# Projecting queries and keys without padding, in a transformer block with two mixtures of experts

## The chip, the cores and the metric

The kernel runs on one NeuronCore of a Trainium2 chip. The metric is device time in microseconds from one launch. Before the change it is 3325.41 us, the median of three runs (3321.82 to 3326.35).

The engines are named as in the profile: PE multiplies matrices (PEld is its weight load), DVE and ACT work elementwise and reduce, POOL also sends indirect transfers, SP only issues transfers. ACT and SP each have a queue of transfers of their own, and each queue works in the order in which it was written.

## The reference, cut to what matters

The input x has 4096 tokens of 256 values. The block is feed-forward, attention, feed-forward, each added to x:

```python
x = x + 0.5 * ffn(layernorm(x))
x = x + attn(layernorm(x))
x = x + 0.5 * ffn(layernorm(x))
```

Attention has 16 heads of 16 values, over all 4096 tokens:

```python
qkv = einsum('bsd,ed->bse', x, qkv_w) + qkv_b      # 3 x 16 heads x 16
scores = einsum('bhqe,bhke->bhqk', q, k) * 0.25
out = einsum('bhqk,bhke->bhqe', softmax(scores), v)
out = einsum('bsd,ed->bse', out, proj_w) + proj_b
```

The feed-forward part routes each token to 4 of 32 experts and adds a shared expert. Everything is fp32.

## The kernel before, in words

The program has five stages: the front of the first layer (`first_front`: normalize, route, shared expert), its experts, the projections to queries, keys and values, attention (into which the front of the second layer is laced in small pieces), and the second layer's experts with the final sums. In `projections` and in `attention` the order on PE, ACT, DVE and SP is the order in which the code is written (`tc.manual_schedule`); POOL's is not fixed so.

**Layout by groups.** A head's 16 values are padded to 32 rows (`HP`), so that four heads fill 128 partitions: a group g of `NG = 4`. The host lays the weights out in this way, with zeros in the padding. Row 16 of each head (`HD`) has a purpose: for keys its weight is 0 and its bias 1.0, for queries it is 0 and later takes a shift, so that the score matmul adds the shift. `kT` holds all keys so padded, 128 x 4 x 4096, in SBUF. The queries go to DRAM as `qd`, one 128 x 512 block for each chunk and group.

**`projections`** works through eight chunks (c) of 512 tokens (`QB`). For a chunk:

- `begin(c)`, on DVE, adds the five results of each token (four experts, shared) with L767, four tiles of 128 tokens, normalizes them (L141 to L167) and gives the rows. Each tile's results come by a fetch on SP (L907, 640 KB); there are six buffers, and the fetch for tile t+6 follows the sums of tile t. POOL then adds the projection's bias to x (L923) and stores it (L926).
- `turned` (L177) transposes the rows on PE; ACT copies them to `xT` (L180).
- `queries_or_keys(c, i, xT)`, i = 0 for queries and 1 for keys: for each of the four groups, two accumulating matmuls (L935), then on ACT the bias and the copy out (L948) and the square (L952). Queries are stored to `qd` from ACT's queue (L950); keys are written straight into `kT`.
- `norms` sums the squares by head with a matmul of 32 output columns for each group (L960); DVE takes the maximum (L967).
- `values` multiplies for v (L974); DVE adds the bias, a tile broadcast to all partitions, and writes v, 17 values for a head, the last one being 1 (L982).
- DVE sums `xT` over the chunk (L1003), for the mean of the keys.

In the code the order is transposes(c), queries(c), `begin(c+1)`, keys(c), norms of the queries, values, norms of the keys. So DVE makes the rows of the next chunk while PE works on this one.

After the last chunk a chain of small steps (L1011 to L1057) finds the mean key (L1019, L1031) and a bound on the scores, from which the shift follows, and a flag. If the flag is set, `take_maxima` finds exact maxima.

**`attention`** goes over 8 chunks of queries, 4 groups and 32 key tiles. At its start DVE clears PSUM banks (L1161), SP loads the first query block (L1165) and the first block of x (L1174), DVE adds the shift (L1170), and PE begins with L1183. Later loads are written two steps into the group before.

Weights for `projections` are loaded on ACT's queue at its start: wqk (L886, 1 MB), wv (L891, two transfers in 64-byte runs), the value bias bv (L898, broadcast), the projection bias (L902).

Of the kernel before, what the change touches and what calls it, by code (L numbers as in the profile page):

```python
# [9 lines left out]
F32 = mybir.dt.float32  # L10
# [49 lines left out]
def kernel(  # L60
# [29 lines left out]
    x1_at = x1[:].rearrange("(t p) d -> p t d", p=P)  # L90
    qd = dram.tile([NQB, NG, P, QB], F32, name="qd")

# [683 lines left out]
    def first_front(layer, keep):  # L776
        n = layer.n
        with (
# [31 lines left out]
            for ch in range(2, nch):  # L810
                load(ch, n)

            routes = [layer.route(ch, xts[ch], pool, pm) for ch in range(nch)]
            xTs = []
# [60 lines left out]
    def projections(layer, side):  # L875
# [4 lines left out]
        with (  # L880
# [3 lines left out]
        ):  # L884
            wqk_sb = pool.tile([P, NC, 2 * NG * P], F32, name="wqk_sb", bufs=1)
            nc.scalar.dma_start(  # L886
                wqk_sb[:], wqkv[:, : 2 * NG * P].rearrange("(c p) e -> p c e", p=P)
            )
            wv_sb = pool.tile([P, NC, NH, HD], F32, name="wv_sb", bufs=1)
            for c in range(NC):  # L890
# [5 lines left out]
                )  # L896
            bv_sb = pool.tile([P, NH, HP], F32, name="bv_sb", bufs=1)
            nc.scalar.dma_start(  # L898
                bv_sb[:].rearrange("p h r -> p (h r)"), bv.to_broadcast([P, NH * HP])
            )  # L900
            bproj_sb = pool.tile([P, D], F32, name="bproj_sb", bufs=1)
# [27 lines left out]
            def queries_or_keys(c, i, xT):  # L929

                squares = []
                for g in range(NG):
                    ps = pm.tile([P, QB], F32, tag="m", name="qk_ps")
                    for cc in range(NC):
                        nc.tensor.matmul(  # L935
                            ps[:],
                            wqk_sb[:, cc, (i * NG + g) * P : (i * NG + g + 1) * P],
                            xT[:, cc, :],
                            start=(cc == 0),
                            stop=(cc == NC - 1),  # L940
                        )
                    bias = bqk_sb[:, i * NG + g : i * NG + g + 1]
                    if i == 0:
                        q = pool.tile([P, QB], F32, tag="q", name="q", bufs=3)
                        part = q[:]
                    else:
                        part = kT[:, g, c * QB : (c + 1) * QB]
                    nc.scalar.activation(part, ps[:], AF.Identity, bias=bias)  # L948
                    if i == 0:
                        nc.scalar.dma_start(qd[c, g], part)  # L950
                    sq = pool.tile([P, QB], F32, tag="sq", name="sq", bufs=2 * NG - 2)
                    nc.scalar.activation(sq[:], ps[:], AF.Square, bias=bias)  # L952
                    squares.append(sq)
                return squares

            def norms(c, i, squares):

                ps = pm.tile([P, QB], F32, tag="m", name="sq_ps")
                for g in range(NG):
                    nc.tensor.matmul(  # L960
                        ps[g * HP : (g + 1) * HP, :],
                        of_head2,
                        squares[g][:],
                        start=True,
                        stop=True,
                    )
                nc.vector.tensor_reduce(norm[:, i, c : c + 1], ps[:], AX.X, ALU.max)  # L967

            def values(c, xT):
                for t in range(0, QT, 2):  # L970
                    ps = pm.tile([P, 2, D], F32, tag="m", name="v_ps")
                    for a in range(2):
                        for cc in range(NC):
                            nc.tensor.matmul(  # L974
                                ps[:, a, :],
                                xT[:, cc, (t + a) * P : (t + a + 1) * P],
                                wv_sb[:, cc].rearrange("p h r -> p (h r)"),
                                start=(cc == 0),
                                stop=(cc == NC - 1),
                            )  # L980
                    for a in range(2):
                        nc.vector.tensor_tensor(  # L982
                            v[:, c * QT + t + a, :, 0:HD],
                            ps[:, a, :].rearrange("p (h r) -> p h r", r=HD),
                            bv_sb[:, :, 0:HD],
                            ALU.add,
                        )

# [3 lines left out]
            for c in range(NQB):  # L992
                xT = pool.tile([P, NC, QB], F32, tag="xT", name="xT")
                for _ in turned(pm, rows, QT, xT, nc.scalar.copy):
                    pass
# [6 lines left out]
                norms(c, 1, k2)  # L1002
                nc.vector.tensor_reduce(sums[:, :, c : c + 1], xT[:], AX.X, ALU.add)  # L1003

# [10 lines left out]
            nc.vector.tensor_scalar(mean_in[:], mean_in[:], 1.0 / T, None, ALU.mult)  # L1015
            ps = pm.tile([P, NG], F32, tag="m", name="kmean_ps")
            for g in range(NG):
                for cc in range(NC):
                    nc.tensor.matmul(  # L1019
                        ps[:, g : g + 1],  # L1020
                        wqk_sb[:, cc, (NG + g) * P : (NG + g + 1) * P],
                        mean_in[:, cc : cc + 1],
                        start=(cc == 0),
                        stop=(cc == NC - 1),
                    )
            mean = small.tile([P, NG], F32, name="mean")
            nc.vector.tensor_add(mean[:], ps[:], bqk_sb[:, NG:])
            nc.vector.tensor_mul(mean[:], mean[:], mean[:])
            ps = pm.tile([P, 1], F32, tag="m", name="mean_ps")
            for g in range(NG):  # L1030
                nc.tensor.matmul(  # L1031
                    ps[g * HP : (g + 1) * HP, :],
                    of_head2,
                    mean[:, g : g + 1],
                    start=True,
                    stop=True,
                )
# [20 lines left out]
        return shift, flag  # L1058

    def take_maxima(kT):  # L1060


        with (
# [3 lines left out]
            for b in range(NQB):  # L1067
                for g in range(NG):
                    q = pool.tile([P, QB], F32, tag="q", name="q")
                    nc.sync.dma_start(q[:], qd[b, g])  # L1070
                    for t in range(QT):
# [25 lines left out]
                        cols = slice(t * P, (t + 1) * P)  # L1097
                        nc.vector.tensor_add(q[:, cols], q[:, cols], tp[:])
                    nc.sync.dma_start(qd[b, g], q[:])

# [48 lines left out]
    def attention(layer, kT, v, shift, keep):  # L1149
# [5 lines left out]
        with (  # L1155
# [5 lines left out]
            nc.vector.memset(pm.all[:, Banks.RING :, :], 0.0)  # L1161

            def load_queries(b, g):
                q = pool.tile([P, QB], F32, tag="q", name="q", bufs=3)
                nc.sync.dma_start(q[:], qd[b, g])  # L1165
                qs[b, g] = q
# [152 lines left out]
    for base, step, sign in ((0, -HP, 1), (HD - 1, HP, -1)):  # L1319
# [8 lines left out]
        )  # L1328
    of_head2 = of_head[:].rearrange("p j r -> p (j r)")

# [108 lines left out]
```

## Time and profile before

| What | Value |
|---|---|
| Median of 3 runs | 3325.41 us |
| The profiled execution | 3322.82 us |
| Its span, first to last instruction | 3321.1 us |
| PE busy | 3061.0 us, 92% |
| ACT busy | 2334.0 us, 70% |
| DVE busy | 979.0 us, 29% |
| POOL busy | 615.0 us, 19% |
| Granted TensorE clock, mean | 0.957 |

The profile comes from one execution. Its page gives the busy time of each engine, groups of instructions by line with count, busy time and mean duration, the idle time before them with what ended it, and the chain of work that ended last. Other views of the same trace give the busy time of each engine in a stretch, the instructions in order of time, and who waited for whom. Times in them count from the start of the span. Idle time of an engine costs nothing unless the work behind it is what ends the kernel, so each stage has to be read on its own.

### The profile page before, as it was taken

The numbers are of one execution on the slowest core, as the hardware profiler recorded it, in microseconds if no ns is written. First come the engines' busy times: TensorE is split into PE (matmuls) and PEld (weight loads), VectorE is DVE, ScalarE is ACT, GpSimd is POOL, SyncE is SP. The second block draws the span as 40 slices with busy tenths as digits, with TensorE's granted clock in tenths as the row PEclk, the third lists the DMA queues.
The fourth block names the chain that finished last, engine by engine and source line by source line (L and its number), as shares of the span: only waits on it lengthen the run. The fifth ranks groups of instructions, "written<-read, shape, count | busy, mean of one in ns | idle before, by whom it ended". The sixth has DMA issues, their size and how long they took to land.

```text
span 3321.1 us, 50114 instructions
## 1 busy us (share of the span) xinstructions
PE 3061.0 (92%) x20183; PEld 1060.6 (32%) x20183; DVE 979.0 (29%) x2837; ACT 2334.0 (70%) x3753; POOL 615.0 (19%) x644
## 2 busy tenths in 40 slices
PE   5769969989999999999999999999999999958990
PEld 3446644422222222222222222222222222225660
DVE  6734447601012112202211210221121122033447
ACT  2112215579999898898999989999998988932220
POOL 3757741100001000100100010010010001015771
PEclk7879989989999999999999999999999999979995
DMA  6358865333100000000000010000000000007878
GB/s 245 132 176 272 275 224 205 122 125 99 59 4 31 17 7 4 27 20 4 30 20 4 12 35 4 7 27 20 4 30 17 7 4 27 7 19 242 275 237 320
DMA packets 131217, 282.21 MB, mean 85 GB/s; under 512 B 23568, under 2 KB 71312, under 8 KB 130576
## 3 DMA queue, kind: packets, MB, share of 16 engines
q1 hardware_dynamic: 83840, 165.84, 14.6%
q0 software_dynamic: 31872, 97.56, 8.4%
q10 hardware_dynamic: 15248, 15.38, 1.4%
q8 instruction: 163, 2.67, 0.3%
q14 instruction: 94, 0.77, 0.1%
HBM read 146.64 MB, written 132.06 MB: 84 GB/s over the span
## 4 chain that ended last, share of the span: by engine, by line
PE 76%; DVE 3%; issue 1%; DMA 0%; SPq 0%; POOL 0%; ACT 0%; DVEq 0%; POOLq 0%
PE banks L1183 33%; PE banks L1201 30%; PE h L720 4%; PE o L742 2%; PE banks L375 2%; DVE xt L767 2%; PE xbt_ps L694 1%; PE banks L1275 1%; PE banks L395 1%; PE banks L230 1%; PE banks L177 0%; PE banks L273 0%; DMA xb<-xg 0%; DMA y<-ys 0%; DVE den L1224 0%
## 5 line engine op out<-in xcount | busy, mean ns | idle before, releaser
L1193 ACT ACTIVATE ex<-banks 128x512 f32<-128x512 f32 (+1 forms) x3223 | 2055.9, 715 | 164.0 <-PE banks L1183 128.5
L1183 PE MATMUL banks<-q,kT 32*128 32x512 f32 x8192 | 1178.3, 641 | 11.2 <-DVE q L1170 9.9
L1201 PE MATMUL banks<-ex,v 128*17 128x512 f32 x8192 | 1079.2, 598 | 0.0
L350 POOL DMA_INDIRECT xg<-xr,sidx x256 | 247.8, 968 | 2275.7 <-DVE beyond L343 2161.7
L1183 PEld LDWEIGHTS banks<-q,kT 32*128 32x128 f32 x8192 | 327.6, 183 | 846.2 <-ACT ex L1193 704.4
L1201 PEld LDWEIGHTS banks<-ex,v 128*17 128x17 f32 x8192 | 136.1, 95 | 778.1 <-issue 777.1
L1221 DVE COPY o<-banks 128x512 f32<-128x512 f32 x32 | 22.1, 692 | 1186.1 <-PE banks L1201 647.9
L750 POOL DMA_INDIRECT ys<-yb,toi x304 | 292.5, 962 | 138.0 <-issue 78.0
L720 PE MATMUL h<-xT,w 128*128 128x512 f32 x512 | 232.1, 596 | 0.0
L700 ACT COPY xT<-xbt_ps 128x512 f32<-128x512 f32 (+1 forms) x112 | 50.6, 452 | 137.4 <-PE xbt_ps L694 105.5
L746 ACT COPY yb<-o 128x512 f32<-128x512 f32 x64 | 37.5, 585 | 136.6 <-PE o L742 94.9
L729 ACT ACTIVATE s<-h 128x512 f32<-128x512 f32 (+1 forms) x112 | 51.5, 460 | 102.5 <-PE h L720 102.5
L720 PEld LDWEIGHTS h<-xT,w 128*128 128x128 f32 x512 | 93.2, 192 | 92.8 <-issue 92.8
L742 PE MATMUL o<-w,hT 128*128 128x256 f32 x512 | 121.1, 379 | 0.0
L935 PE MATMUL qk_ps<-xT,wqk_sb 128*128 128x512 f32 x256 | 113.8, 603 | 1.7 <-ACT xT L180 1.7
L1224 DVE RECIPROCAL den<-den 128x512 f32<-128x512 f32 x32 | 107.3, 3353 | 1.1
L731 DVE TENSOR_TENSOR hT<-s,h 128x512 f32<-128x512 f32 (+1 forms) x112 | 57.8, 516 | 163.1 <-PE h L720 156.8
L742 PEld LDWEIGHTS o<-w,hT 128*128 128x128 f32 x512 | 93.6, 190 | 17.5 <-issue 7.7
L767 DVE SCALAR_TENSOR_TENSOR xt<-y,wk,xt 128x256 f32<-128x256 f32 x192 | 95.1, 495 | 6.9
L694 PE MATMUL xbt_ps<-ident,xb 128*128 128x128 f32 x512 | 71.2, 283 | 28.0 <-DMA xb<-xg 28.0
L698 DVE COPY xT<-xbt_ps 128x512 f32<-128x512 f32 (+1 forms) x112 | 58.1, 518 | 82.2 <-PE xbt_ps L694 61.6
L694 PEld LDWEIGHTS xbt_ps<-ident,xb 128*128 128x128 f32 x512 | 62.3, 145 | 37.0 <-issue 25.0
(221 smaller groups left out, 1761.3 us busy)
## 6 DMA issues: line engine op xcount, KB each, us to landing
y<-ys SPq DMA_DIRECT2D x64, 640.0 KB, 7.1
xb<-xg SPq DMA_DIRECT2D x62, 528.0 KB, 6.4
w<-in_wexp_dram SPq DMA_DIRECT2D x64, 384.0 KB, 4.1
xg<-zeros SPq DMA_DIRECT2D x152, 132.0 KB, 2.2
xg<-zero SPq DMA_DIRECT2D x32, 264.0 KB, 4.4
qd<-q ACTq DMA_DIRECT2D x32, 256.0 KB, 5.0
q<-qd SPq DMA_DIRECT2D x32, 256.0 KB, 2.6
xbb<-xg SPq DMA_DIRECT2D x48, 132.0 KB, 4.6
```

The source lines that it names most:

```text
L350: ins = nc.gpsimd.indirect_dma_start(out=self.xg[:], out_offset=bass.IndirectOffsetOnAxis(ap=self.sidx[:, t0 + t, k : k + 1], axis=0), in_ ...
L375: nc.tensor.matmul(ps[:], ws13_sb[:, c, h0 : h0 + P], xT[:, c, i0 * P : (i0 + QT) * P], start=(c == 0), stop=(c == NC - 1),)
L694: nc.tensor.transpose(tp[:, i * P : (i + 1) * P], xb[:, i, c * P : (c + 1) * P], ident[:])
L720: nc.tensor.matmul(ps[:, : n * P], w[:, (j * NC + c) * H : (j * NC + c + 1) * H], xT[:, c, : n * P], start=(c == 0), stop=(c == NC - 1),)
L742: nc.tensor.matmul(o[:, i, :], hT[:, (i0 + i) * P : (i0 + i + 1) * P], w2, start=True, stop=True)
L750: ins = nc.gpsimd.indirect_dma_start(out=ys[:], out_offset=bass.IndirectOffsetOnAxis(ap=b["toi"][:, i : i + 1], axis=0), in_=yb[:, i, :], ...
L767: nc.vector.scalar_tensor_tensor(xt, y[:, k, :], self.wk[:, t, k : k + 1], y[:, K, :] if k == 0 else xt, ALU.mult, ALU.add,)
L935: nc.tensor.matmul(ps[:], wqk_sb[:, cc, (i * NG + g) * P : (i * NG + g + 1) * P], xT[:, cc, :], start=(cc == 0), stop=(cc == NC - 1),)
L1183: nc.tensor.matmul(pm.all[:, banks[j], :], kT[rows, g, t * P : (t + 1) * P], q[rows, :], start=True, stop=True,)
L1193: nc.scalar.activation(ex[:, i : i + n, :], pm.all[:, k : k + n, :], AF.Exp, scale=SCALE)
L1201: nc.tensor.matmul(acc[j * HP : j * HP + HV, :], v[:, t, g * HG + j, :], ex[:, j, :], start=(t == 0), stop=(t == NT - 1),)
L1224: nc.vector.reciprocal(den[:], den[:])
```

## The change

Queries and keys are projected without padding. Two groups (2h and 2h+1, a half h of `NG // 2 = 2`) share one matmul: the columns of the weights are placed so that rows j*32 to j*32+15 of the output belong to the first group's head j and rows j*32+16 to j*32+31 to the second's.

- The weights come by 16 transfers on ACT's queue, each taking the 64 real columns of a group and half of the contraction.
- The biases are rearranged on DVE with a shuffle and three elementwise steps.
- `qd` is stored by head with 17 rows; row 16 is zeroed by one transfer at the kernel's start. A query block is stored on SP's queue, twice a chunk, and read by four transfers of 17 rows into a tile whose other rows have been cleared; three fixed tiles take turns.
- Keys: ACT first fills the chunk of `kT` with the column that has 1.0 in row 16 of each head, and then eight transfers on SP's queue spread the 16-row pieces into `kT`.
- `norms` uses a matmul of 64 output columns for each half.
- The value bias is added by a matmul with one row of ones; ACT instead of DVE copies v out.
- The sum of `xT` comes from ACT's copy of the transposed rows, by its accumulator.
- `of_both` is built on POOL at the kernel's start.

```diff
-    qd = dram.tile([NQB, NG, P, QB], F32, name="qd")
+    qd = dram.tile([NQB, NG // 2, 2 * HG, HV, QB], F32, name="qd")
...
+            nc.sync.dma_start(
+                qd[:].rearrange("b h k r q -> (b h k) r q")[:, HD, :], zero[:, :QB]
+            )
...
-            wqk_sb = pool.tile([P, NC, 2 * NG * P], F32, name="wqk_sb", bufs=1)
-            nc.scalar.dma_start(
-                wqk_sb[:], wqkv[:, : 2 * NG * P].rearrange("(c p) e -> p c e", p=P)
-            )
+            wqk_sb = pool.tile([P, NC, 2, NG // 2, P], F32, name="wqk_sb", bufs=1)
+            for cc in range(NC):
+                for a in range(2):
+                    for g in range(NG):
+                        h, i = divmod(g, 2)
+                        first_col = (a * NG + g) * P
+                        nc.scalar.dma_start(
+                            wqk_sb[:, cc, a, h].rearrange("p (j i d) -> p i j d", j=HG, i=2)[:, i],
+                            wqkv[
+                                cc * P : (cc + 1) * P, first_col : first_col + P
+                            ].rearrange("p (j r) -> p j r", j=HG)[:, :, :HD],
+                        )
...
+            nc.vector.stream_shuffle(
+                swapped[:], bqk_sb[:], [(r + HD) % HP for r in range(HP)]
+            )
...
+            nc.vector.tensor_scalar(bias_sb[:], first_bias, low_half[:], None, ALU.mult)
+            nc.vector.scalar_tensor_tensor(
+                bias_sb[:], second_bias, high_half[:], bias_sb[:], ALU.mult, ALU.add
+            )
...
+            nc.vector.tensor_scalar(one_row[:], behind[:], SCALE, None, ALU.mult)
...
-            bv_sb = pool.tile([P, NH, HP], F32, name="bv_sb", bufs=1)
+            bv_sb = pool.tile([1, NH, HD], F32, name="bv_sb", bufs=1)
+            nc.scalar.dma_start(bv_sb[:], bv.rearrange("o (h r) -> o h r", r=HP)[:, :, :HD])
...
             def queries_or_keys(c, i, xT):
+                cols = slice(c * QB, (c + 1) * QB)
+                if i == 1:
+                    nc.scalar.activation(
+                        kT[:, :, cols],
+                        zeros[:, 0:1].unsqueeze(2).to_broadcast([P, NG, QB]),
+                        AF.Identity,
+                        bias=one_row[:],
+                    )
                 squares = []
-                for g in range(NG):
+                part = pool.tile([P, NG // 2, QB], F32, tag="q", name="q", bufs=3)
+                for h in range(NG // 2):
                     ps = pm.tile([P, QB], F32, tag="m", name="qk_ps")
                     for cc in range(NC):
                         nc.tensor.matmul(
                             ps[:],
-                            wqk_sb[:, cc, (i * NG + g) * P : (i * NG + g + 1) * P],
+                            wqk_sb[:, cc, i, h],
                             xT[:, cc, :],
...
+                    nc.scalar.activation(part[:, h, :], ps[:], AF.Identity, bias=bias)
                     if i == 0:
-                        q = pool.tile([P, QB], F32, tag="q", name="q", bufs=3)
-                        part = q[:]
-                    else:
-                        part = kT[:, g, c * QB : (c + 1) * QB]
-                    nc.scalar.activation(part, ps[:], AF.Identity, bias=bias)
-                    if i == 0:
-                        nc.scalar.dma_start(qd[c, g], part)
+                        nc.sync.dma_start(qd[c, h, :, :HD, :], part[:, h, :])
...
+                if i == 1:
+                    by_group = kT[:].rearrange("p (h i) t -> p h i t", i=2)
+                    for r in range(0, P, HD):
+                        j, k = r // HP * HP, r % HP // HD
+                        nc.sync.dma_start(
+                            by_group[j : j + HD, :, k, cols], part[r : r + HD, :, :]
+                        )
...
-                for g in range(NG):
+                for h in range(NG // 2):
                     nc.tensor.matmul(
-                        ps[g * HP : (g + 1) * HP, :],
-                        of_head2,
-                        squares[g][:],
+                        ps[h * 2 * HP : (h + 1) * 2 * HP, :],
+                        of_half,
+                        squares[h][:],
...
+                        nc.tensor.matmul(
+                            ps[:, a, :],
+                            ones[0:1, :],
+                            bv_sb[:].rearrange("o h r -> o (h r)"),
+                            start=True,
+                            stop=False,
+                        )
...
-                    for a in range(2):
-                        nc.vector.tensor_tensor(
-                            v[:, c * QT + t + a, :, 0:HD],
-                            ps[:, a, :].rearrange("p (h r) -> p h r", r=HD),
-                            bv_sb[:, :, 0:HD],
-                            ALU.add,
-                        )
+                    t0 = c * QT + t
+                    nc.scalar.copy(
+                        v[:, t0 : t0 + 2, :, 0:HD],
+                        ps[:].rearrange("p a (h r) -> p a h r", r=HD),
+                    )
...
-                for _ in turned(pm, rows, QT, xT, nc.scalar.copy):
+                sums_of = iter([sums[:, cc, c : c + 1] for cc in range(NC)])
+                for _ in turned(
+                    pm,
+                    rows,
+                    QT,
+                    xT,
+                    lambda out, ps: nc.scalar.activation(
+                        out, ps, AF.Identity, accum_out=next(sums_of)
+                    ),
+                ):
                     pass
...
-                nc.vector.tensor_reduce(sums[:, :, c : c + 1], xT[:], AX.X, ALU.add)
...
+    def read_queries(q, b, g):
+        for j in range(HG):
+            nc.sync.dma_start(q[j * HP : j * HP + HV, :], qd[b, g // 2, 2 * j + g % 2])
...
+            q_tiles = [pool.tile([P, QB], F32, name=f"q{i}", bufs=1) for i in range(3)]
+            for q in q_tiles:
+                nc.vector.memset(q[:], 0.0)
+
             def load_queries(b, g):
-                q = pool.tile([P, QB], F32, tag="q", name="q", bufs=3)
-                nc.sync.dma_start(q[:], qd[b, g])
+                q = q_tiles[(b * NG + g) % 3]
+                read_queries(q, b, g)
                 qs[b, g] = q
...
-    of_head2 = of_head[:].rearrange("p j r -> p (j r)")
+    of_both = const.tile([P, 2, HG, HP // HG], F32, name="of_both")
+    nc.gpsimd.memset(of_both[:], 1.0)
+    for base, step, sign in ((0, -1, 1), (HD - 1, 1, -1)):
+        nc.gpsimd.affine_select(
...
+    of_half = of_both[:].rearrange("p i j r -> p (i j r)")
```

The matmuls for the mean key (L1019, L1031) go over the halves in the same way, and `take_maxima` reads its queries by `read_queries` and stores only its row of maxima.

## The prediction

> **What bounds the kernel now.** I read the page's chain first. It says PE 76%, nearly all of it in attention (L1183, L1201), and its pieces reach back only to 678 us, so it says nothing of the projection stage that the change rewrites (about 476 to 681 us):
>
> ```profile
> 678.05 0.02 SPq L1165
> 678.07 0.04 issue
> 678.11 2.72 DMA q<-qd
> ```
>
> The stage is therefore read from the busy time by stretch (columns: PE, weight loads, DVE, ACT, POOL, then granted clock, DMA share, GB/s):
>
> ```profile
> 476.00:497.00 21.00, 1.39 (x5) 0.97 (x6) 13.28 (x42) 0.00 (x0) 0.24 (x1) 0.50 0.84 318
> 539.00:560.00 21.00, 20.76 (x77) 10.17 (x79) 16.77 (x47) 11.28 (x18) 3.11 (x2) 1.00 0.56 202
> 560.00:581.00 21.00, 20.76 (x77) 10.22 (x80) 16.81 (x48) 11.39 (x18) 3.11 (x2) 1.00 0.57 203
> 665.00:682.00 17.00, 4.21 (x36) 3.52 (x32) 5.92 (x21) 1.49 (x2) 0.37 (x1) 0.61 0.14 38
> ```
>
> In steady state PE is busy 20.76 of 21.0 us at full clock: **PE is the bound of this stage**, DVE second with 16.8, ACT 11.3. Ahead of it PE waits 20 us for the first rows; behind it 16 us pass in small serial steps. The groups by line in 476 to 682 us give the terms:
>
> ```profile
> L935 PE MATMUL qk_ps<-xT,wqk_sb 128*128 128x512 f32 x256 | 113.8, 603 | 1.7 <-ACT xT L180 1.7
> L974 PE MATMUL v_ps<-wv_sb,xT 128*128 128x256 f32 x128 | 29.8, 386 | 0.0
> L960 PE MATMUL sq_ps<-sq,of_head 128*32 128x512 f32 x128 | 17.1, 605 | 0.0
> L982 DVE TENSOR_TENSOR v<-v_ps,bv_sb 128x256 f32<-128x256 f32 x32 | 12.1, 420 | 16.8 <-PE v_ps L974 16.8
> L1003 DVE TENSOR_REDUCE sums<-xT 128x2 f32<-128x1024 f32 x8 | 9.7, 1210 | 0.0
> L1019 PE MATMUL kmean_ps<-mean_in,wqk_sb 128*128 128x1 f32 x16 | 3.0, 315 | 2.4 <-DVE mean_in L1015 2.4
> ```
>
> The projection matmuls wait 1.7 us in all, so what PE no longer does comes off the clock until the next engine is reached.
>
> **PE per chunk.** The last chunk in order of time: transposes begin at 644.57, L935 at 645.90, norms at 659.83, values at 660.83, norms at 664.48, end 665.55. So a chunk is 1.33 + 13.93 + 1.00 + 3.65 + 1.00 = 20.91 us. Half the query and key matmuls go: 6.97 instead of 13.93. The value bias adds four K=1 matmuls of 256 columns, eight records; sixteen such records of L974 take 3.65, so +1.82 (a contraction of one row streams as many columns; no row says that it is cheaper). Norms: two matmuls of 64 output columns instead of four of 32. Four of 32 run beside each other (eight records in 1.00 us); if two of 64 do so too, still 1.00; one after another 2 x 0.87 = 1.74, +0.74 twice. I take 1.00, nearest the row. The transposed copy now also sums (no row; 0 to 0.3 us for each of two, partly under the first matmul): +0.15. **PE chunk 15.9 us** (15.8 to 17.4).
>
> **DVE per chunk.** It loses L982 and L1003. One round of sums and normalizing for the next chunk runs from 583.80 to 597.65, 13.85 us; two norm reductions add 1.2. But now there is no slack behind it, and POOL's addition L923 starts as soon as xn is done. Order of time, first chunk:
>
> ```profile
> 496.76 2.37 POOL L923 TENSOR_TENSOR xt<-xt,bproj_sb 128x1024 f32<-128x1024 f32 x1 [28.72 <-PE tp L177]
> 496.95 3.50 DVE L767 SCALAR_TENSOR_TENSOR xt<-y,wk,xt 128x256 f32<-128x256 f32 x3
> ```
>
> Three L767 that otherwise take 1.53 took 3.50: the line's longest instruction is 2.46 us against 0.485, so DVE stood still until POOL was done. In later chunks PSUM reductions and waits lay there and nothing was lost; now the next round's L767 meet it. DVE's loop is 2.45 (end of xn to end of POOL, 597.65 to 600.10) + 13.85 - 0.2 = **16.1 us**, a hair above PE. If the collision vanished, PE's 15.9 would rule.
>
> **ACT per chunk** loses four query/key pairs and its query DMA issues, and gains a fill of kT of 128x2048 (a 512 step is 0.57 us: about 1.9) and two copies for values (0.6 each): 1.2 + 8 x 0.57 + 1.9 + 1.2 = 8.9 us. It is free before the next transposed copy; without that cover the fill would cost 1.9 a chunk.
>
> **SP and the transfers.** Per chunk SP issues 4 fetches, 2 query stores and 8 key transfers, 14 x 0.33 = 4.6 us. The queue is in order, so the fetches of one round now stand behind the next chunk's two query stores (ready 5.6 us into it) and the eight key transfers. A fetch is used about 15 us later and lands in 6.4; cover enough. Bytes per chunk: 4 x 0.655 + 0.5 + 0.5 + 0.5 = 4.2 MB, over 16.1 us 261 GB/s. The 202 of today is demand, as this stretch shows:
>
> ```profile
> 488.00:490.00 2.00, 0.00 (x0) 0.00 (x0) 1.86 (x5) 0.00 (x0) 0.00 (x0) 0.50 1.01 412
> ```
>
> In attention SP loads queries up to two groups ahead (it waits 1269.9 us in all at L1165 for PE to free a tile), so 128 transfers instead of 32 are hidden there.
>
> **The start of the stage.** One 1 MB load becomes 16 of 32 KB in 64-byte runs, on ACT's queue ahead of wv, bv, bproj, and ahead of ACT's first copy at 497.14. The nearest row is eight 32 KB loads at the kernel's start:
>
> ```profile
> 2.35 11.08 ACTq L129 DMA_DIRECT2D wproj_sb<-in_wproj_dram  x8
> ```
>
> 1.39 us each, though one issue takes 0.32. The issues' records name eight completion semaphores, handed out in turn over both queues, so the ninth transfer waits for the first to land, even one of the other queue; SP's list of waits shows it:
>
> ```profile
> SPq L802 <- DMA wproj_sb<-in_wproj_dram: 4.0, 3, 2.7
> ```
>
> 20 issues x 1.39 = 27.7 from 465.28: 493. Against that, the Trainium skill (DMA: Bandwidth & Descriptors, Rules for kernel authors) says to coalesce: under 64 KB one pays mostly overhead. With the roughly 2 us fixed cost that the page fits on another issuing path, paid 20 times, the estimate is 505, 8 us late. I keep the row, and +2 us since the fetches are mixed into the same eight semaphores and the last load still has to land (0 to 8).
>
> First chunk: before, it took 519.20 - 495.61 = 23.6, 2.7 over the steady one (cold clock, first waits). After: 495.6 + 15.9 + 2.6 = 514.1. Six chunks at 16.1 and a last one, with no round of DVE beside it, at 15.9: 626.6, with the late start 628.6. Before 665.55: **-37.0**.
>
> **Behind the stage.** L1003 leaves the path (-1.1), half the L1019 records go (-1.5), a few of L1031 (-0.1): **-2.7**. Then attention begins: before, q<-qd was issued at 678.11, landed at 680.83, PE began at 681.59. Now DVE clears the banks (0.91) and a q tile (0.5, from 1.82 for 2112 columns) first: issue at 679.9 instead of 678.1, and four issues in place of one, +1.0. With the row's 2.6 us to land that makes +2.6. The Trainium skill (DMA: Bandwidth & Descriptors, Why a DMA increments its semaphore by 16 and not by 1) says that a transfer runs on the largest number of engines up to 16 that divides the slowest dimension on both sides: 17 rows would mean one engine, the same for all four. Estimate: 4 x 34.8 KB at 412/16 = 25.8 GB/s is 5.4, after 1.6 from issue to first packet (465.28 to 466.9): landed about 687, +6.4. No 17-row transfer is in the trace; the rule is definite, so I take **+6**. At the kernel's start three more POOL instructions (0.24 for each selection) stand before those that DVE waits for: **+0.3** (0 to 0.6). The store of zero rows is 256 KB beside 11.6 MB of other zeros, hidden; the six small DVE steps that build the biases (0.2 us each) fall into DVE's wait before 482.57; L1060's function isn't run (no row of it).
>
> **Sum:** -37.0 - 2.7 + 6.0 + 0.3 = -33.4 us. The profiled execution took 3322.8 us (span 3321.1): 3289.4. The median shown is 2.6 above it, so the forecast is **3292 us**.
>
> **Rivals.**
> 1. PE's chunk is 17.4 us (norms one after another, or waits between ACT and PE at each hand-over). For it: no row with 64 columns. Against: the 32-column rows overlap. 514.1 + 1.5 + 7 x 17.4 + 2 = 639.4; net -22.6: 3303 us.
> 2. The small weight loads hold ACT until 505: 6 us more, 3298 us. For it: the page's rule, and the second wv load's issue that took 5.83 us. Against: L129.
> 3. The change doesn't do what it says, since transfers hold a chunk at today's 20.9 us: only the tail is left, 3325.4 + 2 - 2.7 + 6.3 = 3331 us. Against: 412 GB/s.
> 4. **Slower:** the eight semaphores, with fetches between the weight loads, leave one load in flight; each of the 20 then costs a landing, 5.4 us (the median of L129's), ACT is held until 573 and all chunks with it: 3325.4 - 33.4 + 74 = 3366 us. It decides from 3.5 us per load (465.3 + 20 x 3.5 = 535, that is 37 us past 497). L129's 1.39 speaks against.
>
> **How the numbers follow.** Forecast 62% (3285 to 3298), rival 1 18%, rival 2 10%, a gain beyond the forecast (queries on many engines, no collision with POOL: -41, 3284) 3%, rival 3 3%, rival 4 4%. About 0.2%, 7 us, is what a measurement of this kernel can tell from no change. Faster: 62 + 18 + 10 + 3 = 93%; within, 3% (rival 3); slower, 4%. The range takes the forecast, rival 2 and most of rival 1: 3284 to 3306.
>
> **What would show it.** L935 with 128 records and a chunk of about 16 us; DVE's L767 line with an instruction of over 2 us in every chunk; ACT's last load issued before 497; four q<-qd landing at about 5 us or more at the stage's end; attention's steps unchanged. Wrong: a chunk above 17.5 us, first matmuls after 505, or PE waiting for q in attention.

## The result, and the profile after

The kernel after takes 3296.41 us (median of four runs, 3293.54 to 3299.01) where the kernel before takes 3324.73 (3321.82 to 3326.35, now with a fourth run): a ratio of 0.9916, 95% interval 0.9898 to 0.9933, or 28.3 us less. The forecast was 3292 us, 33 less. The profiled execution after has a span of 3291.8 us (before 3321.1), so the two profiles differ by 29.3 us, and these are laid out here.

All of it but 0.9 us, by which the stages ahead end earlier, lies in the projection stage and its two ends. PE begins attention at 652.16 us instead of 681.59; from there to the end both kernels take 2639.6 us.

| piece | before | after | difference | forecast |
|---|---|---|---|---|
| first transposes begin | 495.61 | 489.53 | -6.1 | +2 |
| first chunk, to the end of its norms | 23.6 | 21.2 | -2.4 | -5.1 |
| each of seven chunks | 20.91 | 17.26 | 7 x -3.65 = -25.6 | six at 16.1, one at 15.9: -33.9 |
| last chunk's end to attention | 16.04 | 20.66 | +4.6 | +3.3 |
| attention to the end | 2639.5 | 2639.6 | +0.1 | 0 |

The busy time by stretch of the kernel after (columns: PE, weight loads, DVE, ACT, POOL, granted clock, DMA share, GB/s): the wait ahead of the first rows, one chunk, and what follows the last chunk.

```profile
470.00:490.00 20.00, 0.47 (x2) 0.36 (x2) 12.49 (x40) 0.00 (x0) 0.00 (x0) 0.50 0.84 236
545.15:562.41 17.26, 16.92 (x59) 8.09 (x57) 14.04 (x42) 9.17 (x15) 3.22 (x3) 1.00 0.87 261
631.50:652.16 20.66, 1.34 (x14) 1.20 (x13) 5.92 (x21) 2.40 (x3) 0.38 (x1) 0.62 0.12 36
```

PE is still the bound of a chunk, busy 16.92 of 17.26 us at full clock; DVE is busy 14.04. The groups by line say what PE does, and the order of time of one chunk says for how long:

```profile
L974 PE MATMUL qk_ps<-xT,wqk_sb 128*128 128x512 f32 x128 | 58.6, 612 | 3.9 <-ACT xT L1046 3.9
L1022 PE MATMUL v_ps<-wv_sb,xT 128*128 128x256 f32 x128 | 36.2, 405 | 0.0
L1014 PE MATMUL v_ps<-bv_sb,ones 1*128 1x256 f32 x64 | 22.2, 426 | 0.0
```

```profile
545.15 1.09 PE L178 MATMUL tp<-ident,xn 128*128 128x128 f32 x8
546.59 7.13 PE L974 MATMUL qk_ps<-xT,wqk_sb 128*128 128x512 f32 x16 [0.34 <-ACT xT L1046]
553.65 1.08 PE L1001 MATMUL sq_ps<-sq,of_both 128*64 128x512 f32 x4
554.66 0.69 PE L1014 MATMUL v_ps<-bv_sb,ones 1*128 1x256 f32 x2
555.28 1.13 PE L1022 MATMUL v_ps<-wv_sb,xT 128*128 128x256 f32 x4
556.34 0.69 PE L1014 MATMUL v_ps<-bv_sb,ones 1*128 1x256 f32 x2
...
561.40 1.08 PE L1001 MATMUL sq_ps<-sq,of_both 128*64 128x512 f32 x4
```

Transposes and copy take 1.43 us, queries and keys 7.06 (half of before), norms 1.01, **values 6.74**, norms 1.01. The values took 3.65 before:

```profile
660.83 3.72 PE L974 MATMUL v_ps<-wv_sb,xT 128*128 128x256 f32 x16
```

From one bias matmul to the value matmuls behind it is 0.62 us, from there to the next bias matmul 1.06: four times 1.68.

The start, in order of time: ACT's first weight load, the issue of the last scatter (an expert's results going out to DRAM), the first fetch, the first transposes, the first projection. Before, the last four stood at 467.09, 475.82, 495.61 and 497.78.

```profile
464.36 18.53 ACTq L897 DMA_DIRECT2D wqk_sb<-in_wqkv_dram  x16
466.15 0.96 POOL L751 DMA_INDIRECT ys<-yb,toi  x1 [0.30 <-DVE one_row L920]
471.79 18.77 SPq L937 DMA_DIRECT2D y<-ys  x10
489.53 2.21 PE L178 MATMUL tp<-ident,xn 128*128 128x128 f32 x8 [27.96 <-DVE xn L168]
493.27 8.68 PE L974 MATMUL qk_ps<-xT,wqk_sb 128*128 128x512 f32 x16 [1.54 <-ACT xT L1046]
```

The transposes begin 6.1 us earlier than before, the first projection only 4.5: ACT issues its last load at 491.67, makes its first copy at 492.53, and PE waits 1.5 us for it.

Behind the stage the chain of work passes through the query loads:

```profile
643.48 0.31 SPq L1116
...
644.53 6.71 DMA q<-qd
```

From the first issue to the landing are 7.76 us; before, 2.72.

### The profile page after: what moved, and what is told of

It reads as the page before. It is cut to its first block, busy times and chain, and to the rows that moved or that the text cites. A ratio compares the mean times of both kernels' runs of the same rounds, so it can differ in the third digit from the quotient of the medians.

```text
span 3291.8 us, 50155 instructions
## 1 busy us (share of the span) xinstructions
PE 3026.9 (92%) x20043; PEld 1042.0 (32%) x20043; DVE 960.5 (29%) x2806; ACT 2316.8 (70%) x3729; POOL 615.5 (19%) x647
## 4 chain that ended last, share of the span: by engine, by line
PE 76%; DVE 3%; issue 1%; DMA 1%; SPq 0%; ACT 0%; POOL 0%; DVEq 0%; POOLq 0%
PE banks L1252 34%; PE banks L1270 31%; PE h L721 4%; PE o L743 2%; PE banks L376 2%; DVE xt L768 2%; PE xbt_ps L695 1%; PE banks L1344 1%; PE banks L396 1%; PE banks L231 1%; PE banks L178 0%; DMA q<-qd 0%; PE banks L274 0%; DMA xb<-xg 0%; DMA y<-ys 0%
## 5 line engine op out<-in xcount | busy, mean ns | idle before, releaser
L1252 PE MATMUL banks<-q,kT 32*128 32x512 f32 x8192 | 1178.8, 641 | 18.6 <-DVE q L1239 17.6
L743 PEld LDWEIGHTS o<-w,hT 128*128 128x128 f32 x512 | 93.6, 190 | 17.6 <-issue 7.7
L768 DVE SCALAR_TENSOR_TENSOR xt<-y,wk,xt 128x256 f32<-128x256 f32 x192 | 93.1, 485 | 6.9
L695 PEld LDWEIGHTS xbt_ps<-ident,xb 128*128 128x128 f32 x512 | 62.2, 146 | 38.3 <-issue 28.5
L376 PE MATMUL banks<-xT,ws_sb 128*128 128x512 f32 x128 | 67.0, 648 | 4.0 <-DVE u L386 2.8
```

The costliest lines, as they stand in the source:

```text
L376: nc.tensor.matmul(ps[:], ws13_sb[:, c, h0 : h0 + P], xT[:, c, i0 * P : (i0 + QT) * P], start=(c == 0), stop=(c == NC - 1),)
L695: nc.tensor.transpose(tp[:, i * P : (i + 1) * P], xb[:, i, c * P : (c + 1) * P], ident[:])
L743: nc.tensor.matmul(o[:, i, :], hT[:, (i0 + i) * P : (i0 + i + 1) * P], w2, start=True, stop=True)
L768: nc.vector.scalar_tensor_tensor(xt, y[:, k, :], self.wk[:, t, k : k + 1], y[:, K, :] if k == 0 else xt, ALU.mult, ALU.add,)
L1252: nc.tensor.matmul(pm.all[:, banks[j], :], kT[rows, g, t * P : (t + 1) * P], q[rows, :], start=True, stop=True,)
```

## The experiments

Three of the four sets of runs fell on chips where the kernel before takes 3582 to 3590 us, with about 120 us more ahead of the projection stage and 130 more in attention, so each run is compared with its own set, and by the length of a chunk, which is the same on all of them (20.90 before, 17.26 after).

**The kernel after once more**, on the chip on which two of the quicker versions below were run:

> The kernel after unchanged, as the level on the chip of these runs: chunks of 17.26 us, q landing 6.7 to 6.9 us after its last issue, and a ratio to before of 0.992 as on the first chip (0.9916).

Measured: 0.9923 (0.9906 to 0.9939), 3295.88 us, its runs between 3288 and 3300; chunks of 17.26; the chain's `q<-qd` 6.33 us, a little under the 6.7 expected. The result repeats.

### Why the values take 6.74 us

**A full contraction for the bias.**

```diff
-            bv_sb = pool.tile([1, NH, HD], F32, name="bv_sb", bufs=1)
-            nc.scalar.dma_start(bv_sb[:], bv...)
+            bv_sb = pool.tile([P, NH, HD], F32, name="bv_sb", bufs=1)
+            nc.vector.memset(bv_sb[:], 0.0)
+            nc.scalar.dma_start(bv_sb[0:1], bv...)
...
-                            ones[0:1, :],
+                            ones[:],
```

> The kernel after, with the value bias added by a matmul of 128 rows (the bias in row 0, zeros in the others; the same sum) instead of one row. Theory A: PE loses about 0.3 us at each change between a one-row and a 128-row matmul, so values take 5.5 us a chunk instead of 6.74, PE's chunk is 16.0 instead of 17.26, and DVE's round with POOL's addition (16.1) is now next: 8 chunks x 1.2 = 9 us less than the kernel after, about 3287 us. Rival B: four more matmuls simply cost 0.77 us each, whatever their rows: the chunk stays at 17.26, 3296 us.

Measured: values 5.38 us (681.02 to 686.40), chunks of 15.89, first transposes to the last norms' end 134.8 us where a run of the same set with the one-row bias (the one with 16-row queries below) takes 144.2: 9.3 us less. The ratio, 0.9913 (0.9887 to 0.9940), can't resolve that; the order of time does. It shows the same matmuls, now 0.43 to 0.54 us from the bias to the values and 0.86 from there to the next bias (0.62 and 1.06 with one row), and what comes next:

```profile
681.02 0.70 PE L1015 MATMUL v_ps<-bv_sb,ones 128*128 128x256 f32 x2
681.56 1.03 PE L1023 MATMUL v_ps<-wv_sb,xT 128*128 128x256 f32 x4
...
688.16 1.10 DVE L768 SCALAR_TENSOR_TENSOR xt<-y,wk 128x256 f32<-128x256 f32 x1
```

128 rows of mostly zeros are cheaper than one row. The weight loads differ as well: here the load for the values begins at 681.35, beside the bias matmul and 0.21 us ahead of the first value matmul; in the kernel after both begin at 555.28.

DVE comes nearer too: an L768 that takes 0.48 us elsewhere takes 1.10, since it now runs into POOL's addition.

**All bias matmuls of a chunk together.**

```diff
-                for t in range(0, QT, 2):
-                    ps = pm.tile([P, 2, D], F32, tag="m", name="v_ps")
-                    for a in range(2):
-                        nc.tensor.matmul(ps[:, a, :], ones[0:1, :], bv..., start=True, stop=False)
-                        for cc in range(NC): ...
+                tiles = [pm.tile([P, D], F32, tag="m", name="v_ps") for _ in range(QT)]
+                for ps in tiles:
+                    nc.tensor.matmul(ps[:], ones[0:1, :], bv..., start=True, stop=False)
+                for t, ps in enumerate(tiles):
+                    for cc in range(NC): ...
```

> The kernel after with the same one-row bias matmuls, but the four of a chunk are issued together ahead of the eight value matmuls, each into a tile of its own (ACT copies four tiles of 256 columns instead of two of 512). With 128-row bias matmuls the values took 5.38 us, with one-row ones 6.74, so 1.36 us belong to the single row. Theory A: it is paid at the changes between one row and 128 rows, of which there are now 2 a chunk instead of 8: 5.38 + 2/8 x 1.36 = 5.7 us, and a chunk of 16.2 us, near the 16.1 of DVE's round. Rival B: it is a property of each one-row matmul: values stay at 6.7 and the chunk at 17.26.

Measured (3557.47 us, one run): chunks of 16.09 us where tokens and clock held (671.90 to 687.99). Three of the later ones took 17.8 to 19.9: the granted clock fell to 0.91, and in one of them DVE also waited for tokens, up to 3.1 us; so over the stage this run shows no gain (144.1 us). In an undisturbed chunk: bias 1.92, values 3.65, together 5.57.

```profile
681.41 1.99 PE L1013 MATMUL v_ps<-bv_sb,ones 1*128 1x256 f32 x8
683.33 3.72 PE L1022 MATMUL v_ps<-wv_sb,xT 128*128 128x256 f32 x16
```

The one-row matmuls alone cost 0.48 us each, near the 0.456 that the forecast took from L974, and the values behind them are back at 3.65. So the cost isn't in the single row but in the change between contractions of one row and of 128: (6.74 - 5.57) / 6 changes less = 0.2 us each. The 128-row run gives (6.74 - 5.38) / 8 = 0.17, about half of the 0.3 that was expected there, where four changes were counted instead of eight. Theory A holds, rival B falls. The weight load that doesn't run ahead at such a change (0.21 us) would be enough to explain it, but no run separates that.

### Was DVE's round of 16.1 us real?

**No value bias at all.** The bias matmuls are deleted, and the first value matmul starts the sum.

> The kernel after without the value bias (that term is left out of the result). PE's chunk would be 17.26 - 3.09 = 14.2 us. Theory A (the forecast's step on DVE): DVE and POOL then set the chunk at 16.1 us, POOL's addition meets L768, and an L768 of over 2 us is seen in every chunk; 3296 - 8 x 1.2 = 3287 us. Rival B: the collision with POOL is not paid, DVE's own work of 13.9 + 1.2 us sets 15.1: 3279 us. Rival C: PE sets it at 14.2: 3272 us.

Measured: ratio 0.9896 (0.9864 to 0.9927), chunks of 16.09 us (685.68 to 701.77). PE waits 1.2 us in each for `xn`, and the end of DVE's round, POOL's addition and the next sums read:

```profile
685.68 1.74 PE L178 MATMUL tp<-ident,xn 128*128 128x128 f32 x8 [1.21 <-DVE xn L168]
686.51 1.28 DVE L1008 TENSOR_REDUCE norm<-sq_ps 128x1 f32<-128x512 f32 x2
686.69 2.34 POOL L953 TENSOR_TENSOR xt<-xt,bproj_sb 128x1024 f32<-128x1024 f32 x1 [12.68 <-DVE xn L168]
687.71 1.60 DVE L768 SCALAR_TENSOR_TENSOR xt<-y,wk 128x256 f32<-128x256 f32 x1
```

Theory A, but for the length of the L768: the forecast's 16.1 us loop of DVE and POOL exists, and is the bound as soon as PE is quicker. The stretched L768 is 1.60 us, not over 2, since the two norm reductions fill 1.28 us of POOL's 2.34.

**The bias back on DVE**, that part of the change undone: `bv_sb` is loaded to all partitions, the two bias matmuls of a tile and ACT's copy go, and DVE adds the bias as it takes the tile from PSUM, as before.

> The kernel after with this part of the change undone: the value bias added by DVE again as the tiles leave PSUM, no bias matmul, no copy on ACT. PE alone would need 14.2 us a chunk. Theory A: DVE's round sets the chunk: 13.85 of sums and normalizing, 1.28 of norm reductions, 4 x 0.42 of bias additions; these stand between xn and the next sums and cover POOL's addition, so no L768 is stretched: 16.8 us a chunk, still 0.4 less than with the matmul. Rival B: the collision with POOL (1.0 us) is paid on top: 17.8, slower than the matmul. Rival C: PE sets it, 14.2.

Measured (3540.07 us, one run): chunks of 16.05 to 16.51 us from the third on, no L768 over 0.49. Theory A has the order right and is 0.5 us too high: four additions take 1.41 us rather than 1.68, and they lie in POOL's shadow, where DVE would have stood still. So moving the value bias to PE cost the change about 1.0 us a chunk (17.26 against 16.28): by this one profile, and as an estimate, the other parts alone would have been 8 us faster.

### The query loads

```diff
+                if b * NG + g < 3:
+                    for j in range(HG):
+                        nc.sync.dma_start(
+                            q[j * HP : j * HP + HD, :], qd[b, g // 2, 2 * j + g % 2, :HD, :]
+                        )
+                else:
+                    read_queries(q, b, g)
-                read_queries(q, b, g)
```

> The kernel after, with the first load into each of the three query tiles reading 16 rows a head instead of 17 (left out is the row that is zero already unless maxima were taken). Theory A: 17 rows use one DMA engine, which serves the four loads one after another; 16 rows use 16, the wait for q falls from 6.7 us (7.8 from the first issue) to 2.6 to 3, and the time by 4 us to 3292. Rival B: four issues, the fixed cost of a transfer or the store of q just before set the wait: unchanged, 3296 us.

Measured: the wait in the chain is 1.79 us, PE waits 12.8 instead of 17.6 us ahead of its first scores; the ratio is 0.9921 (0.9895 to 0.9946), too wide for 4 us.

```profile
776.40 1.79 DMA q<-qd
```

One row less in each of four transfers, and 5 us are gone: theory A. This agrees with the rule of the Trainium skill (DMA: Bandwidth & Descriptors, Why a DMA increments its semaphore by 16 and not by 1) on which the forecast's +6 rested: 17 rows run on one engine. The trace of the kernel after shows it directly: from 645 to 646 us and from 649 to 651, when the block of x isn't yet or is no longer moving, the DMA share is 0.06 to 0.07 of the 16 engines, at 25 GB/s; the forecast had 25.8.

### The early start

**Before, with the weight load alone changed**: instead of the 1 MB load, sixteen loads of 64-byte runs into the padded tile, whose padding DVE zeroes. And **the kernel before unchanged** on a chip of the same kind, as its level.

> The kernel before with one edit: its 1 MB query and key weight load is replaced by sixteen loads that bring the used 64-byte runs alone, the padding zeroed by DVE. Theory A: the stage starts 6 us earlier in the kernel after since the 1 MB load no longer slows the experts' last scatters and the first token fetches: first fetch issued about 471.8 instead of 475.8, first transposes at about 490 instead of 495.6; 5 to 6 us less than before, 3319 us. Rival B: the early start is due to other parts of the change (fewer rows stored and loaded elsewhere), and sixteen loads on ACT's queue delay its first copy: first transposes at 495.6 or later, 3325 us or more.

> The kernel before unchanged, for the order of time at the start of the stage on another chip, beside the run with narrow weight loads, which had 5.2 us from the last scatter's issue to the first token fetch and 22.2 to the first transposes. Theory A (the wide load slows the scatters and fetches): 8.7 and 28.5 us again, as in the profile of before. Rival B (this chip is quicker there): about 5 and 23 us.

The last scatter's issue, first fetch and first transposes, with narrow loads (and there the first projection), then unchanged:

```profile
599.37 0.96 POOL L750 DMA_INDIRECT ys<-yb,toi  x1 [0.30 <-issue]
604.59 20.65 SPq L915 DMA_DIRECT2D y<-ys  x11
621.60 2.30 PE L177 MATMUL tp<-ident,xn 128*128 128x128 f32 x8 [27.71 <-DVE xn L167]
631.40 16.41 PE L943 MATMUL qk_ps<-xT,wqk_sb 128*128 128x512 f32 x32 [7.50 <-ACT xT L180]
```

```profile
589.69 0.96 POOL L750 DMA_INDIRECT ys<-yb,toi  x1 [0.30 <-issue]
597.49 26.98 SPq L907 DMA_DIRECT2D y<-ys  x12
617.33 2.30 PE L177 MATMUL tp<-ident,xn 128*128 128x128 f32 x8 [34.47 <-DVE xn L167]
```

From scatter to fetch 5.2 us against 7.8, to the transposes 22.2 against 27.6: the narrow loads alone bring the first rows 5.4 us earlier, much as in the change (23.4 against 28.5 in the first two profiles). That half of theory A holds. The other half, 5 to 6 us less in all, does not: ACT has to issue all its loads before it copies the first rows, reaches that copy only at 630.76, and PE stands 7.5 us. This is the second rival of the forecast, in another run. The first chunk then takes 31.8 us where the unchanged kernel takes 22.3, and from the last scatter to the start of attention the narrow version needs 216.3 us against 212.0. Its timed ratio, 0.9991 (0.9978 to 1.0003), shows no clear gain either. Its loads start 1.7 us after the last scatter, since DVE clears the padding first; in the kernel after they start 1.8 us before it, the first fetch still follows after 5.6 us, and PE waits only 1.5 us. That it is the wide load's traffic that holds the scatters up, rather than something else in its issue, is inferred.

### Towards a quicker version

**The bias folded away.** The value bias times the projection's weights is added to the projection's bias once, by one transpose and two matmuls ahead of the stage's first rows; POOL's addition goes out of place, right behind the sums; queries come as four times 16 rows and one load of the four single rows; the first q tile is cleared ahead of the banks.

```diff
-                for _ in normalize(pool, xt, rows, QT):
-                    pass
-                nc.gpsimd.tensor_tensor(xt[:], xt[:], bproj..., ALU.add)
-                nc.gpsimd.dma_start(x1_at[...], xt[:])
+                nc.gpsimd.tensor_tensor(xp[:], xt[:], bproj..., ALU.add)
+                nc.gpsimd.dma_start(x1_at[...], xp[:])
+                for _ in normalize(pool, xt, rows, QT):
+                    pass
...
+        nc.sync.dma_start(
+            q[:].rearrange("(j r) s -> j r s", r=HP)[:, HD, :],
+            qd[b, g // 2].rearrange("(j i) r s -> i j r s", i=2)[g % 2, :, HD, :],
+        )
```

> A version drawn from the runs: no bias in values (the value bias times the projection's weights is added once to the projection's bias, as the weights of a softmax sum to one), POOL's addition out of place ahead of the normalizing so that it meets no L768, queries loaded as four times 16 rows and one load for the four single rows, the first q tile cleared ahead of the banks. Theory: DVE's 13.85 + 1.28 = 15.1 us set the chunk, 8 x 2.1 = 17 us less than the kernel after; q waits about 4 us less, its first issue is 0.9 earlier: 22 us in all, some 3275 us where the kernel after takes 3296, a ratio of about 0.985 to before. Rival B: POOL's addition meets other DVE work and costs the same 1 us: 3283 us. Rival C: PE's hand-overs keep 16 us: 3282 us.

Measured: 0.9904 (0.9888 to 0.9921), less gain than any case named. POOL no longer meets an L768, but chunks are 14.2 to 19.8 us: DVE waits for tokens, and SP, which fetches them, stands still at its key transfers. The waits of both (us in total, times, longest):

```profile
DVE xt L768 <- DMA y<-ys: 13.6, 5, 4.6
```

```profile
SPq L1010 <- DMA y<-ys: 38.5, 21, 3.9
```

SP's queue is in order, and a key transfer waits for a fetch to land before it is issued, so eight of them take 12 to 13 us of SP. The theory failed on a step that I had costed at 8 x 0.33 us.

**Three small edits on the kernel after**: the 128-row bias, the query loads and the clearing as above.

> The kernel after with three small edits: the value bias by a 128-row matmul, queries loaded as four times 16 rows and one load for the four single rows, and the first q tile cleared ahead of the banks. Theory: PE's chunk is 15.9 us (seen with the first edit alone), 8 x 1.37 = 11 us less; q lands about 1.9 us after the last of five issues, with the earlier clearing 5.4 us less; 16 us less than the kernel after. Rival B: SP's queue or the transfers, which a variant with chunks of 15.1 met (tokens arrived up to 4.6 us late), hold this one too: only some 8 us less.

Measured: 0.9885 (0.9865 to 0.9905), 3281.48 us where the kernel after takes 3295.88 in the same set: 14.4 less; PE begins attention 12.8 us earlier. Chunks are 16.09 us, L768 takes 1.60: here too DVE and POOL set the chunk, a little over the 15.9 of PE. Theory, not rival B.

**The folded version with the key transfers on POOL's queue.**

```diff
-                        nc.sync.dma_start(
+                        nc.gpsimd.dma_start(
                             by_group[j : j + HD, :, k, cols], part[r : r + HD, :, :]
                         )
```

> The version without the bias in values again, with two more edits: the key transfers go to POOL's queue instead of SP's, and the two loads for the folded bias too, so that ACT's weight loads begin at once. Theory A: SP's queue in order held the fetches back (eight key transfers took 12 to 13 us of it, most of it in waits for a fetch to land); without them tokens are in time, DVE sets 15.1 us a chunk and first transposes come 23 us after the last scatter instead of 27.6: some 22 us less than the kernel after. Rival B: the DMA engines themselves are the limit (share 0.85 at 16 to 18 us a chunk): chunks stay at 16 to 18 us, 10 us less or nothing.

Measured: 0.9857 (0.9841 to 0.9873), 3274.25 us, the best of all, below before and after. Chunks are 15.09 us, one like the other, and no L768 waits for a token:

```profile
557.75 1.73 PE L178 MATMUL tp<-ident,xn 128*128 128x128 f32 x8 [0.22 <-DVE xn L168]
572.84 1.73 PE L178 MATMUL tp<-ident,xn 128*128 128x128 f32 x8 [0.21 <-DVE xn L168]
```

The same bytes move in less time, so it was SP's order and not the DMA engines: theory A for the chunks (from the fourth on; the first three take 16.7, 14.2 and 14.7). Its other half failed: first transposes come 29.3 us after the last scatter (467.79 to 497.05), not 23. By the profiles, chunks bring 18.7 us, the start loses 6.6, and what follows gains 2.9: PE begins attention 15.0 us earlier. The medians differ by 21.6; the 6.6 us between the two figures lie within the 12 us over which the runs of the kernel after spread.

**The fold behind the first chunk's transposes**, its loads last on ACT's queue:

> The version with keys on POOL's queue, its start mended: in the run before, the bias fold stood on DVE ahead of the first sums, which waited for its load (first sums at 484.06 instead of 476.2), and the stage's first weight load was issued at 472.87 instead of 464.4 behind a tile that came free late; first transposes at 497.05 instead of 490.4. Here the two loads are the last of ACT's queue, as in the kernel after, and the fold comes behind the first chunk's transposes. Theory: first transposes 23 to 24 us after the last scatter again, 3 us for the fold in the first chunk, chunks still 15.1: about 4 us less than that run, a ratio of 0.9845 to before. Rival B: the start is set by something else and the fold costs as much in its new place: 0.9857 again.

Measured: 0.9881 (0.9862 to 0.9900). First transposes come 23.0 us after the last scatter, as the theory says, and chunks are 15.09; but the first chunk takes 25.1 us, as the fold's first step on DVE waits 5.6 us for the bias to land and the next rows are queued behind it. The place was right, the load too late; the time is no better than the run before.

## Why the prediction was right, and what was mis-sized

The mechanism was right: PE is the bound, and half of its query and key matmuls went. That the time fell only 4 us from the forecast is partly luck, since a start 8 us better than forecast met chunks 11 us worse. By its own steps:

- **PE's chunk, 15.9 us: 17.26.** The halved projections (6.97; measured 7.06) and the norms (64 columns do run beside each other: 1.01) were right. The mis-sized term is the **value bias, +1.82, measured +3.09**. "A contraction of one row streams as many columns" is right, 0.48 us each; what the sum lacked is 0.15 to 0.2 us for each change between one row and 128, eight times a chunk. The missing 1.27 us x 8 chunks = 10 us. The chunk thus came out near the 17.4 of the first rival, by a cause that it didn't name.
- **DVE's loop, 16.1 us:** right, but behind PE's, so that the sign I gave for it, a long L768 in every chunk, was missing after (the longest is 0.80). It appears at 16.09 us when the bias is gone. So of the 10 us only (17.26 - 16.09) x 8 = 9 were to be had.
- **The start, +2: measured -6.1.** I asked what sixteen small loads cost on ACT's queue and not what the 1 MB load that they replace had cost others: the last scatters and the first fetch. Of the 6.1, 0.9 come from the stages ahead. The row, 1.39 us a load, was near (sixteen in 18.5 us, the last load at 491.7); the estimate of 505, from the 2 us that the Trainium skill (DMA: Bandwidth & Descriptors, Anatomy of one DMA) fits for a transfer on another issuing path, was wrong here: the sixteen took 1.16 us each.
- **First chunk, 18.5: measured 21.2.** 1.3 of the 2.7 are the bias again, and 1.2 are PE's wait for ACT's first copy (1.54 us, where a later chunk has 0.34): the second rival's cost, small here, 4.0 to 4.2 us in two of the runs above. The repeat's first chunk took 18.7.
- **Small steps behind, -2.7: -3.05. Query loads, +6: +7.7.** The first issue comes 2.5 us later in relation to the steps ahead of it, where 1.8 had been taken, and the landing is 7.76 us after it where 7.1 was.
- **POOL's three instructions at the kernel's start, +0.3:** not seen; the experts end 0.9 us earlier, not later.
- **SP, 4.6 us a chunk: about 16.** Eight key transfers take 11.8 us, mostly in waits for fetches to land. It cost nothing, as the forecast had it, but the cover wasn't the 15 us that I named: at 15 us a chunk it breaks, and at 16 now and then (the run with the bias matmuls together).

Against the forecast of 3289.4 for the profiled execution's time, 3293.5: start -8.1, first chunk +2.7, seven chunks +8.3, behind +1.3; with the +0.3 not seen and the rest rounding, 4.

## What to carry to other kernels

A row added by a matmul of K=1 costs more than its columns when it alternates with full matmuls: put such matmuls together, pad them to full rows, or fold the row into a later bias. When a large load is split or narrowed, ask what it had been slowing besides itself, and what work of the issuing engine stands behind the small ones (PE lost 7.5 us to that with the narrow loads alone); and count an in-order queue's waits, not its issues, before calling it a cover. Each bound that goes shows the next within a microsecond or so (17.3 PE, 16.1 DVE with POOL, then SP's queue), so the price of one cause is only the distance to the next.

## What the runs showed of the hardware

- A change between a matmul of one row and one of 128 rows cost PE 0.15 to 0.2 us each way: a chunk's values took 5.38 us with a bias matmul of 128 rows, 127 of them zeros, and 6.74 with one of a single row.
- Four 17-row transfers of 34.8 KB landed 6.3 to 6.9 us after the last issue, four of 16 rows 1.8 us after it (1.9 to 2.0 with a fifth load for the single rows).
- ACT's copy with a running sum writes that sum by an instruction of its own, 199 ns beside the copy's 593.
- A key transfer on SP's queue, issued behind four fetches, took 1.5 us of the queue where its issue takes 0.59; on POOL's queue seven took 3.5 to 3.7 us.
